# Image 0's VectorE order around its third and fourth row points, and the attention terms moved by 11 copies that follow the eviction of the sums

## The chip, the cores and the metric

One Trainium2 chip (trn2), one of its cores. The metric is device time in microseconds, the median of three runs of the kernel before; one further run was profiled. All data are float32.

## The reference

Two layers, on an input of 4 images, 256 channels, 64 x 64 pixels.

Layer 0 is local attention. A 7 x 7 convolution with dilation 2 takes 256 channels to 128, a 1 x 1 convolution takes them to 49, and a softmax over the 49 gives every pixel a weight for each tap of a 7 x 7 window of dilation 2. Each channel is then the weighted sum of its own pixels in that window:

```python
k = conv7x7(x, w1, dilation=2) + b1          # 256 -> 128
k = conv1x1(k, w2) + b2                      # 128 -> 49
attn = softmax(k, axis=1)
y[b,c,h,w] = sum over u,v of xp[b,c,h+2u,w+2v] * attn[b,7u+v,h,w]
```

Layer 1 whitens y in groups of 64 channels: mean and 64 x 64 covariance over all images and pixels, five Newton steps for its inverse root, and one matrix product for every pixel. It can't begin before all of layer 0 is done.

## The kernel before

**The logits.** The two convolutions are one 7 x 7 convolution to 49 channels. Dilation 2 splits an image into four quarters (row parity x column parity), each a plain convolution. It is done in Winograd's way: along the rows an image is evaluated at the points 0, 1, -1, 2, -2, 1/2 and infinity (indices 0 to 6), and each evaluated row at the same points along the columns. `row_weights(br)` and `weights(b, br, i)` make the weights of row point br, `row_eval` and `col_eval` evaluate the image, all four mostly on VectorE with copies and scalings on ScalarE. `conv_bank` (L471) multiplies on TensorE for one of three banks of column points and evicts the products to the tile `pv` (L501, two buffers). `col_interp` (20 VectorE operations) turns a `pv` into one row of `zz`, `row_interp` (L558) turns the rows of `zz` into the logits `lg`.

In image 0 three row points (1, -1 and 2) go this way. The points 0, -2, 1/2 and infinity are convolved directly by `direct0` (L671, matmuls at L597) into a PSUM tile `acc`, which is evicted into `zz` by ScalarE (L609) or by ScalarE and an add of VectorE (L611, L612). Each `direct0` is 56 matmuls. The points -2 and 1/2 use weights that `keep_weights` has scaled on ScalarE (L306).

The order of image 0 is written out by hand (L684 to L740). While `strict[0]` is set, every VectorE operation made by `add`, `sub` and `madd` is tied behind the one before it (`in_turn`). TensorE's order is that of the program. The other engines' order, and all of VectorE's after L739, is set by a scheduler when the program is built: among instructions that it reckons ready it takes those of high priority first, and the order is then fixed.

**The attention.** For a quarter n (image n // 4, row parity n // 2 % 2, column parity n % 2) `softmax` (L770) turns logits into terms `d`: transposes on TensorE (L780), a maximum on VectorE (L786, L789), exponentials on ScalarE (L794), the division on VectorE (L798 to L807). `move_terms(n)` (L813) copies `d` to `zt` (L837; L839 for half of the copies in the last image), 16 copies of 32 partitions each, and stores `zt` to memory (`sd`, L841). There is one `zt`, so the copies of the next quarter wait for this store. `load_band` (L869) fetches `sd` back into `band` in a skewed form, in three parts, and VectorE transposes each part (L879). There is one `band`.

`first_half(n)` and `second_half(n)` are the two halves of a quarter's weighted sums: `make_block` transposes the image into `xb` (L897, evicted by L905), `weighted_sum` multiplies `xb` by `band` (L926), `store_y` evicts the sums (L945; on VectorE, L943, for one of two in the tail). `turn_y` (L955, evicted to `yt` by L963) and `moments` (L976) gather the covariance. The halves of image b stand between the convolution banks of the next images (`plan`, `gap`), so that TensorE alternates between banks and halves; the last quarters follow without banks between.

In `first_half` the call `move_terms(n + 1)` stands ahead of `store_y`. In `second_half` it is `bands(n + 1)`, which calls `move_terms(n + 1)` and `move_terms(n + 2)`, after it. Neither ties the copies to anything: the scheduler places them wherever it reckons ScalarE free.

Stores of `zt`, loads of `band` and the loads of weights (`wr`, L357) all go through SyncE's queue, which issues them in order.

Of the kernel before, what the change touches and what calls it, by code (L numbers as in the profile page):

```python
# [31 lines left out]
def kernel(  # L32
# [311 lines left out]
    def weights(b, br, i):  # L344

        first = (br, i) not in made  # L350
        made.add((br, i))
        s0 = slot_of[BANKS[i][0]]
        ns = sum(len(taps(bc)) for bc in BANKS[i])
        wt = apool.tile([P, ns, NSK], F32, tag=f"wr{i}", name=f"wr_{b}_{br}_{i}")
        w = {bc: wt[:, slot_of[bc] - s0 : slot_of[bc] - s0 + len(taps(bc))] for bc in BANKS[i]}
        if not first:
            nc.sync.dma_start(wt, gd[br][:, s0 : s0 + ns])  # L357
            return w

        if br == 0:  # L360
            g = [gr0[:, v] for v in range(KS)]
        elif br in kept:

            f = rb[0].rearrange("p q r c w -> p (q r c w)")[:, : KS * NSK]
            if i == 0:
                nc.sync.dma_start(f, kept[br])
            f = f.rearrange("p (v a r k) -> p v a r k", v=KS, a=NCC, r=2)
            g = [f[:, v] for v in range(KS)]
        else:
            g = [gbr[:, v] for v in range(KS)]  # L370
        g = [t.rearrange("p a r k -> p (a r k)") for t in g]
        e, o, e1 = (
            ct.rearrange("p a b -> p (a b)")[:, k * NSK : (k + 1) * NSK] for k in range(3)
        )
        g0 = [g[KS - 1 - a] for a in range(4)]
        g1 = [g[KS - 5 - a] for a in range(3)]
        o0 = {bc: w[bc][:, 0] for bc in w}
        o1 = {bc: w[bc][:, 1] for bc in w if bc != INF}
        if i == 0:
            add(e, g0[0], g0[2])  # L380
            add(o, g0[1], g0[3])
            add(o0[1], e, o)
            sub(o0[2], e, o)
            add(e1, g1[0], g1[2])
            add(o1[1], e1, g1[1])
            sub(o1[2], e1, g1[1])
            nc.scalar.copy(o0[0], g0[0])
            nc.scalar.copy(o1[0], g1[0])
        elif i == 1:
            madd(e, g0[2], 4.0, g0[0])  # L390
            madd(o, g0[3], 4.0, g0[1])
            madd(o0[3], o, 2.0, e)
            madd(o0[4], o, -2.0, e)
            madd(e1, g1[2], 4.0, g1[0])
            madd(o1[3], g1[1], 2.0, e1)
            madd(o1[4], g1[1], -2.0, e1)
            nc.scalar.copy(o0[INF], g0[3])
        else:
            madd(o0[5], g0[0], 2.0, g0[1])
            madd(o0[5], o0[5], 2.0, g0[2])  # L400
            madd(o0[5], o0[5], 2.0, g0[3])
            madd(o1[5], g1[0], 4.0, g1[2])
            madd(o1[5], g1[1], 2.0, o1[5])
            add(o1[5], o1[5], o1[5])
        for bc in BANKS[i]:
            f = SCALE[bc] * (SCALE[br] if br not in kept else 1.0)
            if f != 1.0:
                nc.scalar.mul(w[bc], w[bc], f)
        nc.sync.dma_start(gd[br][:, s0 : s0 + ns], wt)
        return w  # L410
# [134 lines left out]
    def col_interp(b, br, part=None):  # L545
        pv = pvs[b, br]
        pt = {c: pv[:K2, i] for i, c in enumerate(ORDER)}
        outs = phases(zz[:K2, br].rearrange("p q (w two) -> p q w two", two=2))
        cut = lambda t, k: t[:, :, 2 * k : 2 * (k + Q8)].rearrange("p q (b two) -> p q b two", two=2)
        t = it  # L550
        if part is not None:

            t = pvs[b, ROWS[-2]][:, 0]
        interpolate(pt, t[:K2], outs, cut, part)
        if part != 0:
            nc.scalar.copy(outs[3], cut(pt[5], 0))
# [114 lines left out]
    def direct0(br, sr):  # L671
        if br in kept:
            gb = gb5 if br == 5 else gbr
            direct(0, br, sr, acc[:, sr], [gb[:, v, :, sr] for v in range(KS)], xrs[br])
        else:
            u = KS - 1 - 4 * sr - (3 if br == INF else 0)
            w = [tap[:, UPOS[u], v] for v in range(KS)]
            direct(0, br, sr, conv_psum() if br == INF else acc[:, sr], w)
# [24 lines left out]
        bank(1, i)  # L703
    row_weights(3)
    xr = row_eval(0, 3)
    for i in three:
        nxt.update(weights(0, 3, i))
        col_eval(xr, i)
        if i == 0:
            direct0(0, 1)  # L710
            col_interp(0, 1)
    for i in three:
        bank(2, i)
    row_weights(4)
    keep_weights(4)
    xrs[4] = row_eval(0, 4)
    row_weights(5)
    keep_weights(5)
    col_interp(0, 2)
# [7 lines left out]
        "p (q r c w) -> p q r c w", q=Q8, r=2, c=NCC  # L727
    )
    row_eval(0, 5, [rb[0], rb[1], xrs[5]])
    col_interp(0, 3)  # L730
    direct0(4, 0)
    direct0(4, 1)
    row_interp(0, 0)
    direct0(5, 0)
    for i in three:
# [74 lines left out]

    terms, moved, loaded = {}, set(), set()

    def move_terms(n):  # L813

        b, h, pc = n // 4, n // 2 % 2, n % 2
        if n in moved or n >= 4 * B or (b, pc) not in soft_done:
            return
        moved.add(n)
        d = terms[b, pc][:, h].rearrange("p i (u v) -> p i u v", u=KS)
        k = 0  # L820
        for j in range(CR):
            for u in range(CR):

                m, g = divmod(j + u - R, CR)
                ne = 2 if u + CR < KS else 1
                i = d[j * SW : (j + 1) * SW, :, u : u + CR * (ne - 1) + 1 : CR]
                o = zt[g * SW : (g + 1) * SW]
                e = R + KS * m + KS - 1 - u
                o = bass.AP(
                    tensor=o.tensor,  # L830
                    offset=o[:, e].offset,
                    ap=[list(o.ap[0]), [KS * SW, NCH], [(KS - CR) * SW, ne], [1, KS]],
                )

                with tc.high_priority() if n % 4 == 0 else nullcontext():
                    if k % 2 == 0 or b < B - 1:
                        nc.scalar.copy(o, i)  # L837
                    else:
                        nc.vector.tensor_copy(o, i)  # L839
                k += 1  # L840
        nc.sync.dma_start(  # L841
            sd[n % 2].rearrange("(p f) -> p f", p=P),
            zt[:, R : R + NCH * KS].rearrange("p e w -> p (e w)"),
        )
# [91 lines left out]
    def store_y(n, half):  # L936
        yt, pc = where(n)
        ps = y_ps.pop((n, half))
        for cc in range(NCC):
            o = yt[:, cc, half * HALF : (half + 1) * HALF, bass.ds(pc, SW, 2)]  # L940
            with tc.high_priority():
                if tail and cc:
                    nc.vector.tensor_scalar(o, ps[:, cc], pivot[:, cc : cc + 1], None, ALU.add)  # L943
                else:
                    nc.scalar.activation(o, ps[:, cc], AF.Identity, bias=pivot[:, cc : cc + 1])  # L945

    count = [0]
    ybs = {}
# [61 lines left out]
    def first_half(n):  # L1010
        last = open_n.pop() if open_n else None

        def turn(i):
            if last is not None:
                turn_y(last, i)

        for m in (1, 0):
            if (n, m) not in blocks:
                make_block(n, m)
        turn(4)  # L1020
        turn(5)
        weighted_sum(n, 0, 0)
        turn(6)
        make_block(n, 2)
        weighted_sum(n, 0, 1)
        turn(7)
        make_block(n, 3)
        weighted_sum(n, 0, 2)
        make_block(n, 4)
        weighted_sum(n, 0, 3)  # L1030
        weighted_sum(n, 0, 4)

        move_terms(n + 1)
        store_y(n, 0)
        half_done.add(n)
        load_band(n + 1, 0)
        if last is not None:
            moments(last, 1)
            if last % 2:
                move(last // 2)  # L1040
        make_block(n, 6)
        make_block(n, 7)

    def bands(n):

        move_terms(n)
        if n - 1 in half_done:
            load_band(n, 0)
        if n - 1 in done:
            load_band(n, 1)  # L1050
            load_band(n, 2)
            move_terms(n + 1)

    def second_half(n):
        turn_y(n, 0)
        turn_y(n, 1)
        weighted_sum(n, 1, 0)
        weighted_sum(n, 1, 1)
        load_band(n + 1, 1)
        turn_y(n, 2)  # L1060
        make_block(n, 5)
        turn_y(n, 3)
        weighted_sum(n, 1, 2)
        weighted_sum(n, 1, 3)
        weighted_sum(n, 1, 4)
        store_y(n, 1)
        moments(n, 0)
        open_n.append(n)
        done.add(n)
        bands(n + 1)  # L1070
        if n + 1 < 4 * B:
            make_block(n + 1, 1)
            make_block(n + 1, 0)
# [226 lines left out]
```

## Time and profile before

| | |
|---|---|
| three runs | 792.08, 794.63, 799.25 us |
| median | 794.63 us |
| span of the profiled run | 791.8 us |
| TensorE matmul busy | 722.7 us (91%) |
| VectorE busy | 625.9 us (79%) |
| ScalarE busy | 346.4 us (44%) |
| mean granted TensorE clock | 0.972 |

The span has four stretches: loading and weights to 60 us, image 0 from 60 to 205 us, the convolutions of images 1 to 3 together with the attention of images 0 to 2 to about 625 us, and then the rest of the attention and layer 1. A busy share is a mean over all of them. Which engine is waited for in a stretch is read from the timeline of an engine, where a bracket at the end of a line gives its idle time just before the line and what ended it.

### The profile page before, as it was taken

What the parts mean: (1) busy time and instruction counts of PE and PEld (TensorE: products, weight loads), DVE (VectorE), ACT (ScalarE), POOL (GpSimd) and SP (SyncE); (2) the same over time, 40 slices, a digit from 0 to 9 for tenths busy, and PEclk for the clock granted to TensorE, in tenths of its full rate; (3) what the DMA queues carried; (4) which work ended last, traced back from release to release, by engine and by line L of the source; (5) the groups of instructions that cost most, each with busy time, mean ns of one, the idle gap of its engine ahead of it and who ended that gap; (6) DMA issues with size and microseconds to landing.
All of it is one profiled execution on the core that took longest, in us unless ns stands there. A gap on an engine that the chain in (4) does not pass through costs nothing.

```text
span 791.8 us, 18445 instructions
## 1 busy us (share of the span) xinstructions
PE 722.7 (91%) x7444; PEld 547.6 (69%) x7444; DVE 625.9 (79%) x1314; ACT 346.4 (44%) x1018; POOL 34.1 (4%) x46
## 2 busy tenths in 40 slices
PE   4899969799799999989999999896999889998997
PEld 1349653265688887768899958795998768875443
DVE  2696999999888999979896899696979775545443
ACT  1313241125674444378543344765333573422443
POOL 0320000030000010001000100000000000000000
PEclk9999989999899999999999999998999999998999
DMA  8991110033654383048644720542431233381676
GB/s 331 226 297 58 42 72 36 0 107 121 187 182 147 114 313 81 19 153 265 202 124 147 247 66 8 155 161 84 143 87 30 48 113 126 106 298 53 265 301 283
DMA packets 58717, 114.76 MB, mean 145 GB/s; under 512 B 22615, under 2 KB 41736, under 8 KB 57352
## 3 DMA queue, kind: packets, MB, share of 16 engines
q1 hardware_dynamic: 54936, 94.71, 36.2%
q0 software_dynamic: 3696, 18.88, 7.1%
q8 instruction: 59, 0.97, 0.5%
q14 instruction: 26, 0.21, 0.1%
HBM read 66.23 MB, written 47.33 MB: 143 GB/s over the span
## 4 chain that ended last, share of the span: by engine, by line
PE 36%; DVE 29%; ACT 12%; DMA 5%; issue 4%; SPq 1%; DVEq 0%; ACTq 0%
PE y L926 11%; PE cv L491 8%; PE tp L1246 7%; ACT zt L837 6%; DMA sd<-zt 4%; DVE xh L296 3%; PE sig L976 3%; PE tp L897 3%; PE tp L955 3%; DVE zz L296 3%; DVE pv L296 2%; DVE rb L289 2%; ACT d L794 2%; DVE ct L296 2%; DVE pv L292 2%
## 5 line engine op out<-in xcount | busy, mean ns | idle before, releaser
L491 PE MATMUL cv<-xh,wr 128*49 128x128 f32 x4368 | 251.6, 276 | 6.6 <-DVE xh L296 6.5
L491 PEld LDWEIGHTS cv<-xh,wr 128*49 128x49 f32 x4368 | 245.3, 124 | 11.5 <-issue 9.1
L926 PE MATMUL y<-band,xb 128*128 128x224 f32 (+2 forms) x640 | 156.0, 383 | 17.4 <-ACT xb L905 15.2
L926 PEld LDWEIGHTS y<-band,xb 128*128 128x128 f32 x640 | 112.3, 198 | 40.2 <-ACT xb L905 18.1
L837 ACT COPY zt<-d 32x112 f32<-32x112 f32 (+1 forms) x224 | 62.8, 281 | 22.1 <-DMA sd<-zt 13.8
L897 PE MATMUL tp<-ident,slot 128*128 128x128 f32 x256 | 51.1, 303 | 15.0 <-ACT yt L963 15.0
L963 ACT COPY yt<-tp 128x256 f32<-128x256 f32 x128 | 45.4, 375 | 36.7 <-PE tp L955 35.7
L945 ACT ACTIVATE slot<-y,pivot 128x512 f32<-128x512 f32 x53 | 36.5, 736 | 52.3 <-PE y L926 52.3
L501 ACT COPY pv<-cv 113x486 f32<-113x486 f32 (+1 forms) x63 | 29.8, 473 | 63.7 <-PE cv L491 62.4
L897 PEld LDWEIGHTS tp<-ident,slot 128*128 128x128 f32 x256 | 40.3, 206 | 22.3 <-ACT yt L963 16.7
L955 PE MATMUL tp<-ident,slot 128*128 128x128 f32 x256 | 52.2, 300 | 3.6 <-ACT xb L905 1.2
L879 DVE STREAM_TRANSPOSE band<-band 128x960 f32<-128x960 f32 (+1 forms) x48 | 50.9, 1059 | 5.8 <-DMA band<-sd 5.7
L955 PEld LDWEIGHTS tp<-ident,slot 128*128 128x128 f32 x256 | 41.5, 205 | 13.6 <-issue 4.4
L1261 DVE TENSOR_SCALAR out<-tp,scale,beta 128x512 f32<-128x512 f32 x32 | 25.9, 810 | 29.5 <-PE tp L1246 29.5
L794 ACT ACTIVATE d<-tp,mx 128x49 f32<-128x49 f32 x128 | 36.9, 336 | 12.2 <-DVE mx L789 12.1
L1257 ACT ACTIVATE out<-tp,beta,scale 128x512 f32<-128x512 f32 x32 | 24.9, 778 | 32.0 <-PE tp L1246 32.0
L296 DVE SCALAR_TENSOR_TENSOR xh<-ct 128x512 f32<-128x512 f32 x42 | 27.9, 686 | 12.6 <-PE cv L491 12.4
L976 PE MATMUL sig<-yt 128*64 128x65 f32 x1024 | 37.5, 227 | 0.0
L976 PEld LDWEIGHTS sig<-yt 128*64 128x64 f32 x1024 | 33.0, 140 | 6.0 <-issue 4.5
L1246 PE MATMUL tp<-slot,PS 128*128 128x512 f32 x80 | 35.9, 593 | 0.0
L905 ACT COPY xb<-tp 128x256 f32<-128x256 f32 x87 | 30.6, 374 | 12.0 <-PE tp L897 11.2
L597 PE MATMUL cv<-slot,wi 128*49 128x496 f32 (+3 forms) x168 | 34.7, 570 | 0.0
(203 smaller groups left out, 991.7 us busy)
## 6 DMA issues: line engine op xcount, KB each, us to landing
out_dram<-out SPq DMA_DIRECT2D x32, 512.0 KB, 2.6
sd<-zt SPq DMA_DIRECT2D x16, 896.0 KB, 4.3
slot<-in_x_dram POOLq DMA_DIRECT2D x12, 1024.0 KB, 10.0
band<-sd SPq DMA_DIRECT2D x128, 84.0 KB, 2.1
wr<-gd SPq DMA_DIRECT2D x15, 588.0 KB, 4.0
wr<-gd SPq DMA_DIRECT2D x15, 490.0 KB, 3.5
w<-in_L_conv_w_dram SPq DMA_DIRECT2D x4, 1568.0 KB, 11.9
spill<-slot POOLq DMA_DIRECT2D x3, 2048.0 KB, 7.8
```

The source lines that it names most:

```text
L296: return in_turn(STT(o, a, f, b, ALU.mult, ALU.add))
L491: nc.tensor.matmul(cv[h * HB : h * HB + KT, k, sr : sr + n, sc : sc + n], wv[:, sc, sr, cc], xh[bc][:, :n, h * NCC + cc, :n], start=(j == ...
L794: nc.scalar.activation(d[:, h, i], lt[i // NI][:, i % NI, h, :KT], AF.Exp, bias=mx[:, i, h : h + 1], accum_out=s[:, h, i : i + 1],)
L837: nc.scalar.copy(o, i)
L879: nc.vector.transpose(f, f)
L897: nc.tensor.transpose(t[:, cc * P : (cc + 1) * P], xt[:, cc, CR * m : CR * (m + 1), bass.ds(pc, SW, 2)], ident,)
L926: nc.tensor.matmul(ps[:, cc, q0 - half * HALF : q1 - half * HALF, :], xb[:, cc * P : (cc + 1) * P], rhs, start=(k == 0), stop=(k == len(PI ...
L945: nc.scalar.activation(o, ps[:, cc], AF.Identity, bias=pivot[:, cc : cc + 1])
L955: nc.tensor.transpose(t[:, cc * P : (cc + 1) * P], yt[:, cc, CR * i : CR * (i + 1), bass.ds(pc, SW, 2)], ident,)
L963: nc.scalar.copy(yb.rearrange("p a g c -> p (a g) c")[:, :, :GW], t[:, :C].rearrange("p (e c) -> p e c", c=GW),)
L976: nc.tensor.matmul(sig[g * GW : (g + 1) * GW, cc], yb[:, cc, g, :GW], yb[:, cc, g], start=(count[0] == 0 and cc == 0), stop=(count[0] == 4 ...
L1246: nc.tensor.matmul(t, wm[cc], slots[2 * b + pr][:, cc, q * TR : (q + 1) * TR, :].rearrange("p r w -> p (r w)"), start=True, stop=True,)
```

## The change

It has two parts.

**Image 0's order.** After the third row point's first bank, the next operations of VectorE are those that the second bank and the direct convolution of point -2 need: the weights of the second and third bank, and `row_weights(4)`, `keep_weights(4)` and `row_eval(0, 4)`. `col_interp(0, 1)` and `col_eval(xr, 2)` come after them. `direct0(4, 0)` stands between the second and the third bank of the third row point, and `direct0(4, 1)` ahead of `col_interp(0, 3)`. No operation is added or removed.

**The terms.** Copies whose source and target partitions run on together are joined: four of 32 partitions become one of 128, and two pairs become one of 64 each, 11 copies instead of 16. `store_y` returns its last ScalarE eviction, and the copies that ScalarE makes after a half are tied behind it in ScalarE's order (a constraint on the order alone, not a semaphore). `move_terms(n + 1)` moves behind `store_y` in `first_half`. The copies of an image's first quarter, which `soft` starts through `bands(4 * b)`, stay untied.

```diff
-    for i in three:
-        nxt.update(weights(0, 3, i))
-        col_eval(xr, i)
-        if i == 0:
-            direct0(0, 1)
-            col_interp(0, 1)
-    for i in three:
-        bank(2, i)
+    nxt.update(weights(0, 3, 0))
+    col_eval(xr, 0)
+    direct0(0, 1)
+    nxt.update(weights(0, 3, 1))
+    col_eval(xr, 1)
+    nxt.update(weights(0, 3, 2))
     row_weights(4)
     keep_weights(4)
     xrs[4] = row_eval(0, 4)
+    col_interp(0, 1)
+    col_eval(xr, 2)
+    bank(2, 0)
+    bank(2, 1)
+    direct0(4, 0)
+    bank(2, 2)
     row_weights(5)
     keep_weights(5)
     col_interp(0, 2)
...
     row_eval(0, 5, [rb[0], rb[1], xrs[5]])
+    direct0(4, 1)
     col_interp(0, 3)
-    direct0(4, 0)
-    direct0(4, 1)
     row_interp(0, 0)
     direct0(5, 0)
...
+    MOVES = [(0, 0, 4), (2, 0, 2), (2, 2, 2)]
+    MOVES += [(s, j, 1) for s in (1, 3) for j in range(CR)]
-    def move_terms(n):
+    def move_terms(n, after=None):
...
-        for j in range(CR):
-            for u in range(CR):
-                m, g = divmod(j + u - R, CR)
-                i = d[j * SW : (j + 1) * SW, :, u : u + CR * (ne - 1) + 1 : CR]
-                o = zt[g * SW : (g + 1) * SW]
+        for k, (s, j0, nj) in enumerate(MOVES):
+            u = (s + R) % CR
+            m, g = divmod(j0 + u - R, CR)
+            i = d[j0 * SW : (j0 + nj) * SW, :, u : u + CR * (ne - 1) + 1 : CR]
+            o = zt[g * SW : (g + nj) * SW]
...
-                    if k % 2 == 0 or b < B - 1:
-                        nc.scalar.copy(o, i)
+                if k % 2 == 0 or b < B - 1:
+                    ins = nc.scalar.copy(o, i)
+                    if after is not None:
+                        tc.add_manual_dep(ins.ins, after.ins.name, ...)
...
-        move_terms(n + 1)
-        store_y(n, 0)
+        move_terms(n + 1, store_y(n, 0))
...
-        store_y(n, 1)
+        last = store_y(n, 1)
...
-        bands(n + 1)
+        bands(n + 1, last)
```

More of the change, by code (lines that the diff above doesn't have):

```diff
@@ L819, in move_terms @@
         d = terms[b, pc][:, h].rearrange("p i (u v) -> p i u v", u=KS)
-        k = 0
-        for j in range(CR):
-            for u in range(CR):
-                m, g = divmod(j + u - R, CR)
-                ne = 2 if u + CR < KS else 1
-                i = d[j * SW : (j + 1) * SW, :, u : u + CR * (ne - 1) + 1 : CR]
-                o = zt[g * SW : (g + 1) * SW]
[L828 to L835, printed above, removed]
-                    if k % 2 == 0 or b < B - 1:
[L837 to L840, printed above, removed]
+        for k, (s, j0, nj) in enumerate(MOVES):
+            u = (s + R) % CR
+            m, g = divmod(j0 + u - R, CR)
+            ne = 2 if u + CR < KS else 1
+            i = d[j0 * SW : (j0 + nj) * SW, :, u : u + CR * (ne - 1) + 1 : CR]
+            o = zt[g * SW : (g + nj) * SW]
+            e = R + KS * m + KS - 1 - u
+            o = bass.AP(
+                tensor=o.tensor,
+                offset=o[:, e].offset,
+                ap=[list(o.ap[0]), [KS * SW, NCH], [(KS - CR) * SW, ne], [1, KS]],
+            )
+            with tc.high_priority() if n % 4 == 0 else nullcontext():
+                if k % 2 == 0 or b < B - 1:
+                    ins = nc.scalar.copy(o, i)
+                    if after is not None:
+                        tc.add_manual_dep(
+                            ins.ins,
+                            after.ins.name,
+                            mybir.DependencyInfo(
+                                mybir.DependencyClass.NoSync, mybir.DependencyReason.DATA
+                            ),
+                            reason="move_terms",
+                        )
+                else:
+                    nc.vector.tensor_copy(o, i)
         nc.sync.dma_start(
@@ L944, in store_y @@
                 else:
-                    nc.scalar.activation(o, ps[:, cc], AF.Identity, bias=pivot[:, cc : cc + 1])
+                    last = nc.scalar.activation(
+                        o, ps[:, cc], AF.Identity, bias=pivot[:, cc : cc + 1]
+                    )
+        return last
     count = [0]
@@ L1042, in first_half, with bands @@
         make_block(n, 7)
-    def bands(n):
-        move_terms(n)
+    def bands(n, after=None):
+        move_terms(n, after)
         if n - 1 in half_done:
@@ L1051, in bands @@
             load_band(n, 2)
-            move_terms(n + 1)
+            move_terms(n + 1, after)
     def second_half(n):
```

## The prediction

> **What bounds the kernel now.** I read the page first, then the timelines of TensorE, VectorE and ScalarE, then windows over stretches that looked odd.
>
> ```profile
> PE 722.7 (91%) x7444; PEld 547.6 (69%) x7444; DVE 625.9 (79%) x1314; ACT 346.4 (44%) x1018; POOL 34.1 (4%) x46
> ...
> PE 36%; DVE 29%; ACT 12%; DMA 5%; issue 4%; SPq 1%; DVEq 0%; ACTq 0%
> ...
> L837 ACT COPY zt<-d 32x112 f32<-32x112 f32 (+1 forms) x224 | 62.8, 281 | 22.1 <-DMA sd<-zt 13.8
> ```
>
> ScalarE is busy for 44%, yet the chain that ended last is in it for 12%, half of that (6%, about 47 us) in the copies of L837; the store of `zt` is 4% more. So a few ScalarE copies stand where TensorE waits. TensorE's timeline shows where:
>
> ```profile
> 107.66 8.69 PE L491 MATMUL cv<-xh,wr 128*49 128x128 f32 x112 [6.53 <-DVE xh L296]
> ...
> 143.72 12.92 PE L597 MATMUL acc<-slot,gb 128*49 128x512 f32 x56 [3.65 <-DVE zz L289]
> ...
> 210.37 2.50 PE L926 MATMUL y<-band,xb 128*128 128x320 f32 x4 [5.42 <-ACT xb L905]
> ```
>
> ```profile
> 345.80 0.50 PE L897 MATMUL tp<-ident,slot 128*128 128x128 f32 x2 [2.63 <-ACT yt L963]
> 347.61 4.87 PE L926 MATMUL y<-band,xb 128*128 128x320 f32 x12 [1.04 <-ACT xb L905]
> 374.21 0.69 PE L926 MATMUL y<-band,xb 128*128 128x96 f32 x4 [1.78 <-ACT xb L905]
> ```
>
> ```profile
> 502.20 0.50 PE L897 MATMUL tp<-ident,slot 128*128 128x128 f32 x2 [2.48 <-ACT yt L963]
> ...
> 542.17 0.70 PE L897 MATMUL tp<-ident,slot 128*128 128x128 f32 x2 [7.40 <-ACT yt L963]
> ```
>
> The first two gaps lie in image 0. The others end with `xb` or `yt`, small evictions of some 0.37 us; ScalarE's timeline shows what stood ahead of the last one:
>
> ```profile
> 525.66 0.61 ACT L837 COPY zt<-d 32x112 f32<-32x112 f32 x2 [2.69 <-DMA sd<-zt]
> ...
> 535.41 0.61 ACT L837 COPY zt<-d 32x112 f32<-32x112 f32 x2 [4.00 <-DMA sd<-zt]
> ```
>
> The terms of quarters 9, 10 and 11 were all placed ahead of quarter 8's `yt`. The second and third set wait for the store of the one `zt`, and everything behind them on ScalarE waits too.
>
> The windows add two things (columns: busy us of TensorE, weight loads, VectorE, ScalarE, GpSimd; then granted clock):
>
> ```profile
> 210.00:217.00 7.00, 6.63 (x22) 4.89 (x22) 7.00 (x18) 5.71 (x20) 0.00 (x0) 0.66 0.31 123
> 377.50:381.00 3.50, 3.50 (x55) 3.43 (x56) 0.95 (x3) 1.89 (x7) 0.00 (x0) 0.85 1.07 338
> 541.50:548.50 7.00, 6.33 (x40) 5.49 (x42) 3.81 (x8) 3.64 (x10) 0.00 (x0) 0.69 0.08 20
> 90.00:174.00 84.00, 72.41 (x557) 35.98 (x553) 80.64 (x171) 19.89 (x37) 4.96 (x7) 0.94 0.12 49
> ```
>
> After a gap TensorE's clock drops for some microseconds. From 90 to 174 us VectorE is busy for 80.64 of 84 us and its timeline has no named wait: there it is the bound, and TensorE's gaps cost nothing by themselves.
>
> [...]no joined copy is in this trace. [...]the trace has a median of 291, which I use. [...]the stores took 4.3 in the median.
>
> **Part 1, image 0.** VectorE's list keeps its work, so its end (the `pivot` sum at 174.2) does not move: 0. What moves is TensorE. `direct0(4, 0)` needs what VectorE finished at 116.1 us; without the 6.8 us of `col_interp` and 2.1 us of `col_eval` ahead of it that is 107.2, with the 1.34 us scaling on ScalarE about 108. It fills the gap at 101. `direct0(4, 1)` then ends near 133, its add stands ahead of `col_interp(0, 3)` (6.9 us), and `direct0(5, 0)`, held at 143.72 by that add, starts near 136.9. Image 1's first two banks end near 172 instead of 178.7. Now the softmax's transposes wait for the logits (last eviction 174.3 + 0.7 = 175.0): 3.6 us earlier than 178.66.
>
> In the order of the changed kernel's instructions VectorE also takes image 0's maximum ahead of three row-evaluation adds. Maximum at 176.4 instead of 182.2, exponentials (4.4 us) from 179, division by 184.3, then two ScalarE copies (1.3 us) and the 11 term copies to 187.8 instead of 194.6. The store lands at 192.2 instead of 199.1, ahead of need. The first sums now wait for ScalarE's list: the second quarter's exponentials to 197.7 and a `zz` copy that VectorE releases near 203, then two `xb`. That is 204.6 against 210.37: 5.8 us. Half of the slow-clock cost there (6.8 us at half speed cost 3.4) may go too, 1.7. Against it: from 263 to 335 us VectorE is full, so a head start of TensorE lasts only as far as VectorE gives up waits of its own. Those between 204 and 285 are 2.37, 2.80, 2.39, 1.29, 0.37 and 0.79, together 10.0 us; I take half, **-5.0**. This takes in the gap at 234 (1.37 us and a slow clock), where term copies stood ahead of `yt`.
>
> **Part 2, the terms.** One quarter: before 12 x 0.291 + 4 x 0.237 (the two forms' durations) = 4.44 us, after 10 x 0.291 + 0.237 = 3.15, 1.3 us less. In the changed kernel's order no tied copy stands ahead of an eviction of its own half any more.
> - 345 us, quarter 4's untied copies ahead of quarter 3's `yt`: 11 instead of 13, and 3 fewer ahead of `xb`: 5 x 0.281 = **-1.4**. 502 us, the same for quarter 8: **-1.4**.
> - 374 us: quarters 5 and 6 no longer stand ahead of `xb`: -1.78, and no slow clock (3.4 us at half speed cost 1.7): **-3.5**. 393 us: 0.66 less the usual 0.26: **-0.4**.
> - 542 us: -7.40. The slow clock: what follows from 542.17 to 546.5 takes 2.7 us where it is undisturbed (578.4 to 581.1): -1.6. Together **-9.0**.
> - Last image: ScalarE 8 copies to 6, VectorE 8 to 5, of which one set stands on the path: **-0.6**.
> - New: behind each tied set stands the eviction of a bank, up to 9 x 0.291 = 2.6 us late. Its `pv` has a second accumulator, and 7 to 12 us of matmuls run before it is needed. The store comes later too: copies end 5.2 us after the sums, store 4.3, loads 2.1, transpose 1.2, 12.8 us; quarter 5's first sum comes 31 us after (405.9 - 374.9). The wait in SyncE's queue delays weights by 2 to 4 us; the loads I followed have 5 us to spare. Nought if all is hidden, 9 sets x 2.6 = 23.4 if none is: I take **+2**.
>
> Sum: -5.0 - 1.4 - 1.4 - 3.5 - 0.4 - 9.0 - 0.6 + 2 = -19.3, so 794.6 - 19.3 = **775.3 us**.
>
> **Rivals.** (a) VectorE takes it back. From 290 to 340 and from 440 to 490 us it is 98% busy (48.9 of 50); if its new order gives image 0's lead back (+5.0) and half of the 9.0 at 542 (+4.5): 784.8. For: the chain is in VectorE for 29%. Against: 6.46 us of waiting for TensorE at 551. (b) More is freed: all 10.0 us of VectorE's waits (-5.0), no new waits (-2), the slow clock gone at 350 (-1.7): 766.6. (c) The tie becomes the wait: 23.4 us of late evictions and one late weight load (4.0) instead of +2: 794.6 - 21.3 + 27.4 = 800.7, slower. Against it stand the slacks above.
>
> **Chances.** Forecast 0.60, (a) 0.17, (b) 0.14, (c) 0.09. The range reaches past (a) and (b), 764 to 788, and leaves out (c). Faster by over 1% (under 786.7): forecast, (b) and two thirds of (a), 0.85; within 1%: the rest of (a) and half of (c), 0.10; slower 0.05.
>
> **What would show it.** Right: no gap at TensorE's `yt` of quarter 8, `direct0(4, 0)` near 108 us, first sums near 205, L837 near 156 copies and 45 us. Wrong: joined copies much longer than 0.29 us; gaps of TensorE before L491 with a `pv` eviction as releaser; VectorE waiting for `band`.

## The result, and the profile after

The changed kernel takes 769.82 us (median of 4 runs, 768.59 to 772.88), beside 793.95 us for the kernel before, the ratio 0.969 with a 95% interval of 0.964 to 0.975. A second set of runs, on which the later experiments rest, gave 771.57 us (6 runs, 770.71 to 774.24) beside 793.24, ratio 0.972 (0.969 to 0.975). The change is worth 22 to 24 us.

The page of the changed kernel, in the lines that answer to those shown of before (busy time, chain of waits, the group of term copies, which is now line 843):

```profile
PE 714.1 (93%) x7444; PEld 542.8 (71%) x7444; DVE 623.6 (81%) x1302; ACT 327.1 (43%) x950; POOL 34.2 (4%) x46
...
PE 38%; DVE 37%; ACT 6%; issue 4%; DMA 2%; SPq 1%; DVEq 0%; ACTq 0%
...
L843 ACT COPY zt<-d 32x112 f32<-32x112 f32 (+2 forms) x156 | 44.9, 288 | 1.7
```

ScalarE's part of the chain has halved, from 12% to 6%, and DMA's has gone from 5% to 2%. The time went to VectorE, 29% to 37%. The 156 copies take 44.9 us, and they wait for 1.7 us in all, where it was 22.1. By shapes (partitions x elements), 64 x 112 and 32 x 112 both take 292 ns in the mean, and 128 x 56 takes 250, where 32 x 56 took 240 in the kernel before: here a wider copy cost 0 and 10 ns more. That it costs nothing more was the author's estimate in the prediction, from the copies of 32 partitions in the trace of before.

TensorE's timeline of the changed kernel (idle time before the line, and what ended it, in brackets). In this profiled run everything after 60.8 us stands 2.9 us earlier than in that of before for a reason that lies ahead of the change:

```profile
104.51 11.59 PE L597 MATMUL acc<-rb,gbr 128*49 128x512 f32 x56 [1.76 <-DVE rb L296]
...
172.20 1.44 PE L783 MATMUL tp<-ident,slot 113*128 113x113 f32 x8 [2.18 <-ACT slot L579]
...
201.99 1.34 PE L941 MATMUL y<-band,xb 128*128 128x320 f32 x4 [1.99 <-ACT xb L920]
...
333.47 0.51 PE L912 MATMUL tp<-ident,slot 128*128 128x128 f32 x2 [1.89 <-ACT yt L981]
334.88 3.18 PE L941 MATMUL y<-band,xb 128*128 128x320 f32 x12 [0.63 <-ACT xb L920]
...
445.64 4.87 PE L941 MATMUL y<-band,xb 128*128 128x320 f32 x12 [1.77 <-ACT xb L920]
...
519.94 0.51 PE L912 MATMUL tp<-ident,slot 128*128 128x128 f32 x2 [1.11 <-ACT yt L981]
```

With the 2.9 us added, `direct0(4, 0)` starts at 107.4, the softmax's transposes at 175.1 and the first sums at 204.9. The gap of 7.40 us ahead of quarter 8's `yt` is gone; the 1.11 at 519.94 stands eight matmuls later, where the kernel before had none. In this profile the first 12 sums behind the gap at 333 run at a granted clock of 1.00 (3.18 us), where it was 0.65 (4.87 us) in the kernel before.

The starts of equally numbered matmuls in two runs tell where the time went. Below, **lead** is how much earlier such a matmul starts than in the kernel before, counted from the one at 60.8 us, so that what lies ahead of the change drops out. The times over the leads are those of the kernel before. The second column adds up VectorE's idle times that a named instruction or transfer ended, from 198 to 298 us of each run's own time. Only one profiled run stands behind each row. The two rows of the changed kernel are of one and the same program and differ by up to 3.5 us, so a smaller difference between two single entries says little.

| run | VectorE's waits from 198 to 298 | lead at 296 | 355 | 413 | 504 | 550 | 623 |
|---|---|---|---|---|---|---|---|
| before | 10.01 | | | | | | |
| changed | 1.05 | 8.7 | 11.5 | 14.3 | 14.3 | 22.2 | 21.2 |
| changed, again | 2.13 | 6.9 | 8.7 | 11.4 | 12.5 | 18.7 | 17.7 |
| order alone | 5.78 | 4.4 | 6.7 | 2.5 | 2.4 | -0.2 | -0.1 |
| terms alone | 6.69 | 3.5 | 6.2 | 9.0 | 9.0 | 16.9 | 16.0 |
| 11 copies alone | 8.01 | 2.0 | 3.1 | 5.0 | 5.3 | 7.0 | 7.0 |
| tie alone | 6.77 | 3.4 | 3.4 | 6.7 | 6.3 | 13.3 | 9.7 |
| changed, not tied | 6.44 | 4.5 | 8.0 | 4.4 | 5.7 | 8.1 | 8.0 |
| changed, 16 copies | 5.32 | 4.6 | 6.9 | 6.6 | 6.0 | 14.7 | 12.7 |
| changed, add late | 7.12 | 1.8 | 4.5 | 7.3 | 7.2 | 15.2 | 14.2 |
| changed, first quarters tied | 1.90 | 8.2 | 12.3 | 10.9 | 13.8 | 19.1 | 13.5 |
| changed, `zz` on GpSimd | 2.31 | 6.5 | 7.5 | 11.3 | 12.1 | 21.5 | 9.8 |
| terms alone, `zz` on GpSimd | 7.63 | 1.9 | 2.9 | 6.7 | 7.4 | 16.8 | 5.1 |
| changed, `zz` on VectorE | 0.67 | 8.8 | 12.7 | 16.5 | 17.3 | 26.6 | 26.5 |

Read the second and third column together: the lead at 296 us is what VectorE has given up of its own waiting, within 1.2 us in every row (changed: 10.01 - 1.05 = 8.96, lead 8.7; terms alone 3.3, lead 3.5; 11 copies alone 2.0, lead 2.0). So VectorE sets the pace of that stretch. After it the steps at 345, 374, 502 and 542 us follow, where TensorE's gaps in the kernel before end with ScalarE's `yt` and `xb`.

### The profile page after: what moved, and what is told of

Its sections match the earlier page's. It is cut to its first block, busy times and chain, and to the rows that moved or that the text cites. A ratio compares the mean times of both kernels' runs of the same rounds, so it can differ in the third digit from the quotient of the medians.

```text
span 767.1 us, 18362 instructions
## 1 busy us (share of the span) xinstructions
PE 714.1 (93%) x7444; PEld 542.8 (71%) x7444; DVE 623.6 (81%) x1302; ACT 327.1 (43%) x950; POOL 34.2 (4%) x46
## 4 chain that ended last, share of the span: by engine, by line
PE 38%; DVE 37%; ACT 6%; issue 4%; DMA 2%; SPq 1%; DVEq 0%; ACTq 0%
PE y L941 11%; PE cv L491 8%; PE tp L1262 7%; DVE xh L296 4%; DVE pv L296 3%; DVE rb L296 3%; PE tp L912 3%; DVE ct L296 3%; PE sig L994 3%; PE tp L973 3%; DVE zz L296 2%; DVE ct L289 2%; DVE pv L292 2%; DVE band L894 2%; ACT zt L843 2%
## 5 line engine op out<-in xcount | busy, mean ns | idle before, releaser
L491 PE MATMUL cv<-xh,wr 128*49 128x128 f32 x4368 | 250.2, 275 | 0.0
L491 PEld LDWEIGHTS cv<-xh,wr 128*49 128x49 f32 x4368 | 244.0, 124 | 5.1 <-issue 2.7
L941 PE MATMUL y<-band,xb 128*128 128x224 f32 (+2 forms) x640 | 150.9, 375 | 12.3 <-ACT xb L920 10.6
L941 PEld LDWEIGHTS y<-band,xb 128*128 128x128 f32 x640 | 109.4, 193 | 33.5 <-ACT xb L920 13.0
L973 PEld LDWEIGHTS tp<-ident,slot 128*128 128x128 f32 x256 | 41.3, 205 | 14.2 <-issue 4.4
L843 ACT COPY zt<-d 32x112 f32<-32x112 f32 (+2 forms) x156 | 44.9, 288 | 1.7
L920 ACT COPY xb<-tp 128x256 f32<-128x256 f32 x87 | 30.5, 376 | 12.2 <-PE tp L912 11.4
## 6 DMA issues: line engine op xcount, KB each, us to landing
w<-in_L_conv_w_dram SPq DMA_DIRECT2D x4, 1568.0 KB, 11.4
```

The costliest lines, as they stand in the source:

```text
L491: nc.tensor.matmul(cv[h * HB : h * HB + KT, k, sr : sr + n, sc : sc + n], wv[:, sc, sr, cc], xh[bc][:, :n, h * NCC + cc, :n], start=(j == ...
L843: ins = nc.scalar.copy(o, i)
L941: nc.tensor.matmul(ps[:, cc, q0 - half * HALF : q1 - half * HALF, :], xb[:, cc * P : (cc + 1) * P], rhs, start=(k == 0), stop=(k == len(PI ...
L973: nc.tensor.transpose(t[:, cc * P : (cc + 1) * P], yt[:, cc, CR * i : CR * (i + 1), bass.ds(pc, SW, 2)], ident,)
```

## The experiments

**Each part alone.** The kernel before with the new order of image 0, which is the first part of the change's diff, and all else as it was:

> Image 0's new order alone, the terms as before (16 untied copies). Theory of the prediction: TensorE reaches image 0's softmax about 3.6 us and the first sums about 5.8 us earlier, and VectorE lets some of it live: 785 to 789 us beside 794. Rival, VectorE takes it back: the lead at the first sums is there, but it is gone where VectorE is full (300 to 335 us), 792 to 795. Rival, the two parts only work together: under 2 us.

Measured 793.82 us, ratio 0.999 (0.997 to 1.001): nothing. The number fits both rivals. The lead speaks against the first of them: it lives through the stretch where VectorE is full (4.4 us at 296, 6.7 at 355), and is down to 1.9 only at 374. TensorE's and ScalarE's timelines of that run:

```profile
364.41 0.51 PE L900 MATMUL tp<-ident,slot 128*128 128x128 f32 x2 [2.34 <-ACT yt L966]
```

```profile
361.10 2.39 ACT L840 COPY zt<-d 32x112 f32<-32x112 f32 x8
...
368.00 1.51 ACT L840 COPY zt<-d 32x112 f32<-32x112 f32 x5 [2.13 <-DMA sd<-zt]
369.54 0.37 ACT L966 COPY yt<-tp 128x256 f32<-128x256 f32 x1
```

TensorE comes earlier, but now eight copies of quarter 5 stand ahead of the `yt` that it needs. They wait for nothing; they cost a gap of 2.34 us, where the kernel before had none, and some 1.6 us in slower matmuls behind it (the four sums at 366.70 take 2.16 us, those at 360.60, before the gap, 1.24). Then the copies of quarter 6 wait for the store of quarter 5, ahead of the next `yt` and `xb`; TensorE's two gaps there, 1.14 and 0.77 us, are together little more than the 1.78 that it had there before. So most of what image 0 brought is lost behind copies on ScalarE. Of the 2.4 us that are left at 504, 1.7 go into slower sums behind the gap at 502 (nine of them take 4.30 us, where twelve took 3.18 in the kernel before), which one profile doesn't settle, and the gap of 7.40 us at 542 is still there, at 7.87.

The terms alone, which is the rest of the change's diff, with image 0's order as before:

> The terms' 11 tied copies alone, image 0's order as before. Theory of the prediction: the gaps of TensorE at 345, 374, 502 and above all 542 us shrink, about -16, and the one at 234 with its slow clock goes too, -3: 775 to 780 us beside 794. Rival, the tie becomes a wait: gaps of TensorE before the convolutions' banks, with the eviction of a bank as releaser, 785 or more.

Measured 774.54 us, ratio 0.975 (0.972 to 0.977), 19.4 us faster, just past the 775 to 780 that the prediction's theory gave. By the medians the order adds the rest, 3 to 5 us, though the intervals of the ratios overlap; a run further down, with one add late, tests the order against the changed kernel itself. What TensorE and ScalarE do at 242 us without the new order:

```profile
243.18 0.66 PE L909 MATMUL tp<-ident,slot 128*128 128x128 f32 x2 [2.79 <-ACT yt L978]
```

```profile
241.99 0.32 ACT L556 COPY zz<-pv 113x144 f32<-113x144 f32 x1 [3.64 <-DVE pv L296]
242.21 0.65 ACT L457 COPY xh<-rb 128x512 f32<-128x512 f32 x1
242.76 0.36 ACT L978 COPY yt<-tp 128x256 f32<-128x256 f32 x1
```

The copy of L556 is not one of terms. It is the last step of `col_interp`, the copy of a `pv` that VectorE has finished, and it waits for VectorE at the head of ScalarE's queue while `yt` stands behind it. TensorE is idle for 2.79 us there and is slower behind it (four sums take 2.34 us there, 1.24 in the changed kernel); the lead falls from 8.6 to 3.9. In the changed kernel VectorE is done in time, and the lead falls by 0.7.

The two halves of the terms' change:

```diff
 # 11 copies alone: no tie, and the call ahead of store_y as before
-        move_terms(n + 1, store_y(n, 0))
+        move_terms(n + 1)
+        store_y(n, 0)
-        bands(n + 1, last)
+        bands(n + 1)
 # tie alone: 16 copies, tied and placed as the change has them
-    MOVES = [(0, 0, 4), (2, 0, 2), (2, 2, 2)]
-    MOVES += [(s, j, 1) for s in (1, 3) for j in range(CR)]
+    MOVES = [((u - R) % CR, j, 1) for j in range(CR) for u in range(CR)]
```

> 11 copies instead of 16, but untied and where the kernel before has them; image 0's order as before. If the number of copies is what stood in the way, most of the terms' gain is here: 778 to 782. If their place is (copies of later quarters, and the waits for the store of the one zt, ahead of yt and xb), the wait at the yt of quarter 8 stays at 3 us or more and the gain is some 8 us: 784 to 788.

> 16 copies, tied behind the eviction of the sums as the change ties them; image 0's order as before. If their place is what matters, nearly all of the terms' gain but the 1.4 us twice at the untied first quarters: 777 to 781. If the number is, 786 or more.

Measured 784.22 us for the 11 copies (ratio 0.987, 0.984 to 0.989) and 783.33 for the tie (0.985, 0.982 to 0.988): 9.7 and 10.6 us, which add up to what both bring together (19.4). The first lies where it was expected if the copies' place is what matters, the second between its two theories: neither number nor place does it alone. They are worth about the same, though in different places. At 542 us the 11 copies alone leave a gap of 4.63 us, and the tie alone one of 0.38, yet with the tie alone 16 copies hold ScalarE longer (0.60 + 2.62 + 1.40 us for the set at 535.86, where 11 took 0.54 + 2.73 in the changed kernel), and a gap of 2.05 stands at the next half (TensorE's timeline of the tie alone):

```profile
548.02 4.87 PE L937 MATMUL y<-band,xb 128*128 128x320 f32 x12 [2.05 <-ACT xb L916]
```

**One part taken out of the changed kernel.** These ran beside the changed kernel itself, but for the one with 16 copies, which ran later:

> The changed kernel once more, beside the next three on the same chip. All theories: 0.969 to 0.971 of the kernel before, about 769 to 771 us. It is the base from which the next three are counted.

771.57 us, ratio 0.972. Without the tie:

```diff
-                    if after is not None:
+                    if False:
```

> The changed kernel without the tie (11 copies, called where the change calls them, image 0's order new). Theory 1, the copies that wait for a store swallow image 0's lead: the order is worth nothing here, as in the run of the order alone, and the time is that of the joined copies alone, 784 us (783 to 786), with xb or yt again behind copies of zt that wait for the store of zt. Theory 2, the gains of the parts add: joined copies alone less 5 us for the order, 779 us. Theory 3, the later place of the call is enough and the tie does nothing: 770 us.

Measured 781.07 us, ratio 0.984 (0.980 to 0.988), 9.5 us slower than the changed kernel. Theory 3 falls: the later place of the call is not enough, the scheduler moves the copies forward again. Between theories 1 and 2 the time lies in the middle. Its lead says that theory 1's mechanism is at work: it has 8.0 us at 355 and 4.4 at 413. TensorE waits 1.97 us at 360 behind copies of quarter 5, and 3.11 at 364 behind those of quarter 6, which wait for a store. ScalarE's timeline shows this second wait:

```profile
363.63 0.56 ACT L843 COPY zt<-d 128x56 f32<-128x56 f32 x2 [2.67 <-DMA sd<-zt]
364.21 0.37 ACT L981 COPY yt<-tp 128x256 f32<-128x256 f32 x1
```

With 16 copies, tied (the `MOVES` of the tie alone):

> The changed kernel with 16 copies of 32 partitions instead of 11, tied and placed as in the change. Theory 1, the order's lead lives as soon as no copy of terms waits for a store ahead of yt or xb, the tie does that alone, and the joined copies are worth what they were between the tie alone and the terms (8.8 us): 778 us (777 to 780). Theory 2, the longer sets of copies swallow the order's lead, as the untied ones did: 783 us, as the tie alone.

Measured 780.73 us, ratio 0.982 (0.978 to 0.987), and the interval (777 to 784) holds both theories. The lead at 296 is 4.6 us, much nearer to the 3.4 of the tie alone than to the changed kernel's: by then the 16 copies have cost part of the order's lead. Joining is worth some 8 us here too.

With `direct0(4, 1)` behind `col_interp(0, 3)` again:

```diff
-    direct0(4, 1)
     col_interp(0, 3)
+    direct0(4, 1)
```

> The changed kernel with direct0(4, 1) behind col_interp(0, 3) again. Theory 1, image 0's lead comes from direct0(5, 0) being released earlier, and lives on: the softmax's transposes stand 3.6 us later than in the changed kernel, the first sums some 3 to 6 us later, and 3 to 5 us of it are still there at the end: 773 to 775 us. Theory 2, VectorE is the bound of image 0 and of 263 to 335 us, and swallows a lead of TensorE: the start moves, the end by less than 1 us: 770 us.

Measured 777.67 us, ratio 0.980 (0.977 to 0.983): 6.1 us slower than the changed kernel, for two calls exchanged and no work added. Theory 1 holds, and was too low. The transposes stand 5.5 us later (3.6 expected), VectorE waits 7.12 us up to 298, and at 243 it has not done its `pv` when quarter 1's `yt` is due; the wait is the one seen with the terms alone, and longer (ScalarE's timeline of this run):

```profile
242.84 0.32 ACT L556 COPY zz<-pv 113x144 f32<-113x144 f32 x1 [8.14 <-DVE pv L296]
```

With this one exchange undone the rest of the new order brings nothing: the run is no faster than the terms alone with the old order (ratio 0.980 beside 0.975). So the order's worth needs the early add.

**What is left.** The change leaves the first quarters' copies untied, and gaps of 1.89 and 0.54 us before `yt` there. Tied as well, for images 1 and 2:

```diff
-        if pc == 0:
+        if pc == 0 and b in (0, B - 1):
             bands(4 * b)
```

> The changed kernel with the copies of the first quarters of images 1 and 2 tied as well, behind the last sums of the quarter before. Theory 1, what is left at these two places (1.89 + 0.63 us of TensorE at 333, 0.54 + 0.61 at 485, less the usual 0.25 each) is due to the untied copies alone: 2.5 to 4 us faster than the changed kernel, 766 to 767.5 us. Theory 2, the terms then come too late: copies end some 10 us later, store and loads take 6.4 us more, so TensorE waits for band of quarters 4 and 8, 2 to 6 us slower, 772 to 776 us. Theory 3, the gap is only passed on to the next wait for VectorE: 770 us.

Measured 777.22 us, ratio 0.979 (0.976 to 0.981): 5.7 us slower. Theory 2 has the direction, but only part of the cause. Both gaps do go (the lead at 347 rises by 3.7 us instead of 1.2), but three other waits come in or grow on TensorE:

```profile
355.14 2.36 PE L941 MATMUL y<-band,xb 128*128 128x320 f32 x4 [2.22 <-DVE band L894]
...
510.62 1.65 PE L491 MATMUL cv<-xh,wr 128*49 128x128 f32 x26 [2.62 <-DMA wr<-gd]
...
540.28 0.70 PE L912 MATMUL tp<-ident,slot 128*128 128x128 f32 x2 [2.61 <-ACT yt L981]
...
541.67 5.54 PE L941 MATMUL y<-band,xb 128*128 128x320 f32 x12 [0.27 <-ACT xb L920]
```

Quarter 4's terms come too late for its first sums. At 510 a load of weights is late, as the prediction feared of SyncE's queue for the tie as such: it was issued at 506.17, behind the loads of quarter 8's `band`, where the changed kernel issues it from 494.45 on. The third wait costs most, since the 12 sums behind it take 5.54 us instead of 3.18: between 550 and 623 the lead falls by 5.6 us, in the changed kernel by 1.0. There a `zz` copy waits 7.05 us for VectorE ahead of `yt`; that VectorE is late there because of the tie was not tested. By the time, leaving these copies untied is right.

The other gaps left (389.76 and 519.94) end as the terms alone did at 243: a `zz` copy of L556 waits for VectorE ahead of `yt`. Two runs take that copy off ScalarE, onto GpSimd:

```diff
-            nc.scalar.copy(outs[3], cut(pt[5], 0))
+            nc.gpsimd.tensor_copy(outs[3], cut(pt[5], 0))
```

> The changed kernel with the copy of pv to zt's neighbour zz (L556, 21 times, after VectorE has done a pv) on GpSimd instead of ScalarE. Theory 1, this copy waits for VectorE at the head of ScalarE's queue and holds the pv and yt evictions behind it: the gaps of TensorE before yt at 389.76 (0.86) and 519.94 (1.11) go, with the slow clock behind them, 2 to 4 us faster than the changed kernel: 767 to 769 us (ratio 0.967 to 0.970). Theory 2, VectorE is the bound there and the wait only moves to the next bank: 771 us. Theory 3, GpSimd's copies are long or slow VectorE down: over 773 us.

> The change to the terms alone (image 0's order as before), with the copy of L556 on GpSimd. It asks why the order is worth nothing alone and some 5 us with the terms. Theory 1, without it the same copy waits for VectorE at 242 us and holds quarter 1's yt back (2.79 us and a slow clock, 4.7 in all): with the copy out of ScalarE's queue most of this comes back, 770 to 771.5 us, and the order is worth under 2 us more. Theory 2, the order's worth is TensorE's and VectorE's earlier start itself: 774 to 775 us, as the terms alone.

Measured 781.83 us (ratio 0.983, 0.979 to 0.986) and 786.46 (0.988, 0.985 to 0.991), both slower than without this edit. GpSimd's and ScalarE's timeline of the first:

```profile
521.83 21.17 POOL L556 COPY zz<-pv 113x144 f32<-113x144 f32 x2 [23.20 <-DVE pv L296]
```

```profile
542.77 0.56 ACT L501 COPY pv<-cv 113x486 f32<-113x486 f32 x1 [12.67 <-POOL zz L556]
```

Most of the 21 copies take 0.3 to 0.7 us, one stood for 20.9, and the next bank's `pv` waited for it, with an idle time of 8.04 us on TensorE. That alone costs some 11 us of lead in either run, so their times say nothing of the theories. Their first half does: with the terms alone and the `zz` copy away, the lead still falls from 8.1 to 2.4 us at 243, since the next thing in ScalarE's queue that needs VectorE now waits, with `xb` behind it (ScalarE's timeline of that run):

```profile
247.19 0.53 ACT L408 ACTIVATE wr<-wr 128x392 f32<-128x392 f32 x1 [3.03 <-DVE wr L289]
247.62 0.35 ACT L917 COPY xb<-tp 128x256 f32<-128x256 f32 x1
```

ScalarE did not wait for GpSimd there: its idle times between 239 and 250 us ended with a transfer (1.83 us), with VectorE (3.03) and with TensorE (0.72). So at 243 it is VectorE that is late, and which copy waits for it matters little. This is against theory 1 of the terms with `zz` on GpSimd, and for the order's worth being VectorE's lead. The same edit with VectorE instead of GpSimd (`nc.vector.tensor_copy`), on the changed kernel:

> The changed kernel with the copy of L556 on VectorE, which writes the pv it copies. On GpSimd one such copy stood for 21 us, so that run could not answer its question; here no engine waits for another between pv and zz. Theory 1, the wait for VectorE at the head of ScalarE's queue is what is left of TensorE's gaps before yt at 389.76 and 519.94: they go, and 21 x 0.30 = 6.3 us more of VectorE, most of it beside other work, cost less: 766 to 769 us (ratio 0.966 to 0.969). Theory 2, ScalarE waits for VectorE in any case, at the next copy or scaling that VectorE releases, and the 6.3 us come on top where VectorE is full (image 0 has three of the copies, 0.9 us): 772 to 775 us.

Measured **764.48 us** (6 runs, 763.14 to 769.71), ratio 0.965 (0.961 to 0.968), 29.3 us faster than the kernel before and 7.1 faster than the changed kernel by the second set of its runs (5.3 by the first, where the intervals overlap). Theory 1, a little better than its range. Its page and its copies:

```profile
PE 713.0 (93%) x7444; PEld 542.3 (71%) x7444; DVE 626.7 (82%) x1323; ACT 322.5 (42%) x929; POOL 34.1 (4%) x46
...
PE 47%; DVE 34%; ACT 4%; issue 3%; DVEq 0%; ACTq 0%
```

```profile
L556 DVE COPY zz<-pv x21: 285/295/298, 111.2 to 588.9; 113x144 f32<-113x144 f32 x21
```

The copies take 21 x 0.295 = 6.2 us by their durations, which overlap those of their neighbours; VectorE's busy time rises by 3.1 us. Still the kernel is faster, because `pv` and `yt` evictions no longer queue behind a copy that VectorE has not released: the gaps at 389.76 and 519.94 are gone. Of those at the untied first quarters, the one of 1.89 at 333 is gone as well (0.62 stays at 334), and the ones at 485 have grown (1.27 and 0.62 at 483). This version beats both kernels.

## Why the prediction was right, and where it was off

The forecast was 775.3 us, the runs gave 769.8 and 771.6. All its main steps happened, and the sum of the leads, 19.3 to 21.7 us, is close to the forecast's 19.3. The medians differ by 22 to 24 us; some of what is more may lie ahead of 60.8 us, where nothing was changed and single runs differ by up to 2.9 us. By its own terms, from the leads of the two profiled runs of the changed kernel (the first and the second value):

| term of the sum | predicted | measured |
|---|---|---|
| image 0 and the gap at 234 (lead at 331) | 5.0 | 8.7, 6.9 |
| 345 us | 1.4 | 2.8, 1.8 |
| 374 and 393 us | 3.9 | 3.9, 3.9 |
| new waits (398 to 488) | -2.0 | -3.1, -1.4 |
| 502 us | 1.4 | 1.9, 1.3 |
| 542 us | 9.0 | 7.9, 7.9 |
| all else (509, and from 550 on) | 0.6 | -0.4, -1.1 |
| sum | 19.3 | 21.7, 19.3 |

- **Image 0.** The steps were right: transposes 3.6 us earlier (3.6 and 3.5), first sums 5.8 (5.5 and 3.7), `direct0(4, 0)` at 108 (107.4). The size was off by 2 to 4 us, the largest error of the sum. The step that failed is the term "together 10.0 us; I take half": VectorE gave up 8.96 and 7.88 of these 10.01 us, not 5. The rule behind it, that a head start lasts as far as VectorE gives up waits, held in every row of the table. Of these waits 5.2 us ended with TensorE's banks and 3.7 with loads of `band`; in the changed kernel both came earlier. The prediction gave no reason to halve them. Windows from 204 to 285 us show it, before and changed (busy us of TensorE, weight loads, VectorE and so on):

```profile
204.00:285.00 81.00, 73.38 (x950) 65.86 (x947) 70.64 (x161) 45.00 (x131) 0.57 (x1) 0.94 0.50 166
```

```profile
204.00:285.00 81.00, 77.14 (x1050) 70.86 (x1050) 80.66 (x194) 42.77 (x114) 3.95 (x3) 1.00 0.55 185
```

  VectorE goes from 70.64 to 80.66 of 81 us, and TensorE's clock from 0.94 to 1.00. The order and the terms each free a part of it alone (10.01 to 5.78, 10.01 to 6.69), and both together nearly all.
- **345 us.** The gaps fell by 2.63 + 1.04 - 1.89 - 0.63 = 1.15 us, close to the 1.4 of the step. The rest is 4.87 - 3.18 = 1.7 us of slow clock behind them (0.65 before, 1.00 in the changed kernel), which the prediction had put into rival (b). In the second profile the sums were slow there too (4.25 us), and the step is 1.8.
- **374, 393, 502 us** were right within 0.5 us. The half speed that the prediction counts with is what the windows of the kernel before show: a granted clock of 0.50 from 208.0 to 214.5 us and from 375.5 to 378.5.
- **542 us.** 7.40 of gap, and 1.6 of clock (0.58 from 542.0 to 546.5 us in the kernel before), less the new gap of 1.11, is 7.9. The gap did go to nought, as predicted. What was not foreseen is the new one, a `zz` copy waiting for VectorE. In the kernel before this copy stood at 539.47, in the midst of the copies of terms, and had nothing to wait for any more.
- **New waits.** TensorE's matmuls of the banks (L491) waited for nothing (0.0 us in 4368), so neither a late eviction of a bank nor a late load of weights held them, and what the +2 was taken for did not come about. That its size fits is luck. What was lost there in the first profile is a wait for VectorE through `zz` at 389.76 (0.86 us), which the second one has too, and 1.7 us of slow clock at 445 (0.65 in the 4.87 us of the 12 sums), which it has not. This is a small part of rival (a): VectorE takes a little back, through ScalarE's queue.
- **Rival (b)** came in part: its first term nearly whole (8.96 and 7.88 of the 10.01), its slow clock at 350 in one profile of the two, its absence of new waits in neither.
- **Rival (c)** had no case here. The tie turns into a wait only when the first quarters are tied as well, and then by the late load of weights that it named (2.62) and by a late `band` (2.22), which the prediction had among its signs of being wrong.

That the order and the terms don't add was not in the prediction. It gave image 0 a term of its own, 5.0 us with the gap at 234 in it, and the order alone was expected to bring 5 to 9; it brought none, because most of the freed time ended behind copies of terms on ScalarE. At 296 us the leads of the two parts do add (4.4 and 3.5, together 8.7 and 6.9); it is after that point that one part of the change keeps what the other frees.

## What to carry to other kernels

Here ScalarE, busy for 44%, held TensorE, busy for 91%, through its queue (for 7.40 us at 542): list what stands ahead of each small eviction that the busiest engine waits for, and ask of each whether it can itself wait. Take the ones that wait out of that queue (tie them behind the eviction, or give them to the engine that they wait for), even where this adds work to a fuller engine (3.1 us more of VectorE here, and the kernel 5 to 7 us faster). A lead won in one stretch was worth here what the full engine of the next stretch gave up in waits, so add those up, and don't halve them without a reason in the trace.

## What was not expected of the hardware

- A GpSimd copy of 113 x 144 elements takes 0.41 us in the median and took 20.9 in one place. For that time VectorE had gone from one operation with two operands to the next; the copy's end came 0.25 us after VectorE began a transpose with one operand (VectorE's timeline of the changed kernel with `zz` on GpSimd):

```profile
542.49 1.17 DVE L894 STREAM_TRANSPOSE band<-band 128x960 f32<-128x960 f32 x1
```

  Another copy in this run stood for 5.52 us from 219.38 on, and it too ended 0.25 us after the start of such a transpose (224.65). With the terms alone and `zz` on GpSimd the long one is there as well: two copies from 526.81 on took 21.18 us. What held them was not shown.
- The same idle time does not always cost the clock. Before the same 12 sums (445 us in the changed kernel) TensorE was idle for 1.76 us in the kernel before, and for 1.77 and 1.78 in the two profiles of the changed one. The sums then took 3.18, 4.87 and 3.18 us, the first at a granted clock of 1.00, the second at 0.65 (TensorE's timelines of the kernel before, and of the second profile of the changed one):

```profile
462.58 3.18 PE L926 MATMUL y<-band,xb 128*128 128x320 f32 x12 [1.76 <-ACT xb L905]
```

```profile
451.43 3.18 PE L941 MATMUL y<-band,xb 128*128 128x320 f32 x12 [1.78 <-ACT xb L920]
```

  A slow clock in one profile behind such a gap is not yet a cost of the kernel.
